# A Mamba mixer and gated MLP on one core: mixer input loaded by feature, x and B turned by DRAM blocks and VectorE

## The chip, the cores and the metric

The kernel runs on one core of one Trainium2 chip. The metric is device time in microseconds: the time of one execution as the device reports it, median of the runs. A profile of one execution (the hardware profiler's record) goes with it. TensorE is called PE, its weight load PEld, VectorE DVE, ScalarE ACT, GpSimd POOL and SyncE SP; SP issues nearly all DMAs.

## What is computed

`u` has 4 sequences of 1024 tokens with 256 features. Everything is float32.

```python
x = u
x = x + layernorm(mixer(layernorm(x)))
x = x + layernorm(mlp(layernorm(x)))

def mixer(u):                       # 8 heads of 64, state of 128
    z, xBC, dt = split(u @ in_proj) # 512 | 512 + 128 + 128 | 8
    x, B, C = split(silu(causal_conv4(xBC)))    # depthwise, over tokens
    dt = softplus(dt + dt_bias)
    dA = dt * -exp(A_log)
    # a linear recurrence over tokens, worked out in chunks:
    #   state = exp(dA) * state + dt * x B^T ;  y = C state + D * x
    y = y * silu(z)
    return rmsnorm(y) * norm_weight @ out_proj

def mlp(x):                         # 4-bit weights with scales per 32
    return (gelu(x @ Wg.T) * (x @ Wu.T)) @ Wd.T     # width 2048
```

The recurrence needs the transposed form of some operands. Projections and the convolution leave x, B and C by feature: features on partitions, tokens along the free axis. Two products of a chunk contract over tokens, so x (scaled by `dt`) and B are needed with tokens on partitions.

## The kernel before, in words

**Segments and chunks.** The 4096 tokens are cut into nine segments (line 26): two of 256 tokens, then seven of 512. A segment is cut into chunks of 128 tokens. For each segment `mixer(s)` (736) makes a list of steps and `ffn(s)` (1137) another.

**A planner sets the order.** No instruction is issued where the code stands. `Recorder.add` (181) notes each operation with what it reads and writes. `Recorder.issue` (288) then simulates the five engines, with a cost for each operation (`weigh`, 253), a rate and a fixed time for DMAs (344 to 349), a margin after each producer (`slack`, 142; 1.5 us after a DMA), and pools of buffers. At each step it takes, among the operations that can start soonest, the one of lowest rank (395), and so writes down a fixed order for each engine. That order is emitted at line 379, which is why every row of the profile says L379. On the chip each engine runs its list strictly in order and waits at each semaphore. Mixer steps of segment s + 2 rank ahead of the MLP of segment s, so that the two are interleaved.

**The mixer before the change.**
- `norm_in` (751): statistics of each token by DVE (`stats_of`, 594), the reciprocal deviation by POOL (`rstd_of`, 587), then for each chunk DVE writes `xn`, PE transposes its two halves into an `a` bank, and ACT copies the banks to `xnT`, which holds the normalized input by feature.
- `step_sizes` (767) and `decays` (818): dt, and the decay factors. The running sums by token go to DRAM (`rows`) and come back spread over partitions as `e` and `r`.
- `feature_pair` and `gate_pair` (1024, 1018), in segments from s = 4 on: input projections with seven products in place of eight (`pair`, 990), a Strassen scheme on 256x256 blocks. A pair occupies two of the four `f` banks of PSUM. The weights' sums come from DRAM (`win<-mstock`). Earlier segments use plain matmuls (`features`, 860).
- `convolve` (869): one ACT pass and three DVE passes from the bank into `xc`, then a tanh and a product that make silu.
- `inner(i)` (900), for each chunk: `e` and `r` are loaded, and exponentiated. PE transposes the four feature blocks of x into one bank (935 and 936), and DVE makes `xdt` and `xw` from it (939, 942). PE multiplies B by C, transposes B into the same bank (958), and ACT copies it to `bt` (960).
- `scan(i)` (1029): output from the state, update of the state from `bt` and `xw`, output within the chunk from `xdt` and `e`. Then `gated`, `way_out` and `turned` (1066 to 1111) end in `xfT`, the MLP's input by feature.

**The MLP.** `widen_pair` (1213) computes gate and up with the seven-product scheme (`seven`, 1189): PE writes into two `f` banks, ACT copies two halves on, DVE adds twice (`f<-f,sums`), PE goes on. This ring is the bulk of the work. Gelu and the product with up write the tile `big`; `narrow` (1221) multiplies by Wd into the `d` banks. Blocks of the weights' sums (1792 KB each) are fetched from DRAM by `fetch` (1171), `wide<-stock`, two buffers.

**Queues.** All loads and stores named here stand in SP's one list. SP waits at an issue until the buffer is free, and what is behind it in the list waits too.

Of the kernel before, what the change touches and what calls it, by code (L numbers as in the profile page):

```python
# [14 lines left out]
ALU = mybir.AluOpType  # L15
PSUM = bass.MemoryType.PSUM

P = 128
# [9 lines left out]
TMAX = 512  # L28
# [8 lines left out]
SIDE = 2  # L37
OUT = True
SEVEN = 4
MASKED = -2.0 ** 100  # L40

ATANH = (2.000000007877749, 0.6666631593507933, 0.400248537235466, 0.2796141883358907,
# [126 lines left out]
class Recorder:  # L169
# [118 lines left out]
    def issue(self, tc, rank, patience):  # L288


        steps = self.steps
        follows = [[] for _ in steps]
        for st in steps:
            st.missing = len(st.before)
            st.ready = st.floor
            st.rank = rank(st)
            for b in st.before:
                follows[b.at].append(st)
        open_ = {e: [] for e in self.ENGINES.values()}
        table = "exp"  # L300
        for st in steps:
            if not st.missing:
                open_[st.engine].append(st)
        free = {e: 0.0 for e in open_}
        wires = 0.0
        bundle = None
        order = []
        while len(order) < len(steps):
            best = None
            for e, sts in open_.items():  # L310
                when = {}
                for st in sts:
                    starts = [b.pool.may_start(b) for b in st.buffers]
                    if None not in starts:
                        when[st] = max(starts + [st.ready, free[e]])
                if e == "ACT" and when:


                    now = min(when.values())
                    other = [st for st in when if st.table not in (None, table)]  # L320
                    for st in other:
                        when[st] += SWITCH
                    if len(other) < len(when):
# [12 lines left out]
            t, st = best  # L336
            e = st.engine
            st.start = t
            if e == "ACT" and st.table:
                table = st.table  # L340
            turn = min(PORT, max(0.0, free["POOL"] - t)) if st.port and t < EARLY else 0.0
            free[e] = t + st.busy + turn
            st.end = free[e] + st.after
            if st.name == "dma_start":
                if st.bytes > 20000:
                    wires = max(free[e], wires) + st.bytes / (230.0 if st.repeats else 350.0)
                    st.end = wires + 1700.0
                else:
                    st.end = free[e] + 1900.0
            for b in st.buffers:  # L350
                if b.slot is None:
                    b.pool.take(b)
                b.left -= 1
                b.until = max(getattr(b, "until", 0.0), st.end)
                if not b.left:
                    b.pool.free.append((b.until, b.slot))
            if e == "PE":
                bundle = st.bundle
            open_[e].remove(st)
            order.append(st)  # L360
            for f in follows[st.at]:
                flows = f.before[st]
                if e == "PE" and f.engine == "PE":
                    r = st.start
                elif f.engine != e:
                    r = st.end + slack(e, f.engine)
                elif flows:
                    r = st.end
                else:
                    r = st.start  # L370
                f.ready = max(f.ready, r)
                f.missing -= 1
                if not f.missing:
                    open_[f.engine].append(f)
        self.order = order
        with tc.manual_schedule():
            for st in order:
                real = lambda a: a.on(a.buf.pool.slots[a.buf.slot]) if isinstance(a, View) else a
                getattr(getattr(self.nc, st.queue), st.name)(  # L379
                    *[real(a) for a in st.args], **{k: real(a) for k, a in st.kwargs.items()})  # L380
# [25 lines left out]
def mamba_ffn_kernel(  # L406
    ctx: ExitStack,
    tc: tile.TileContext,
    u: bass.AP,
    w_in: bass.AP,  # L410
    conv_w: bass.AP,
    conv_b: bass.AP,
# [18 lines left out]
    def pool(name, shape, k=1, ahead=2, of=None, dtype=F32):  # L431
        of = of or sb
        return Pool([of.tile(shape, dtype, name=f"{name}{j}") for j in range(k)], ahead)

    def fixed(name, shape, dtype=F32):
        return pool(name, shape, dtype=dtype).get()

    def given(ap):
        return Pool([ap]).get()

    u, w_in, conv_w, conv_b, dt_bias, a_log, d_skip, norm_w, w_out = map(
        given, (u, w_in, conv_w, conv_b, dt_bias, a_log, d_skip, norm_w, w_out))
    g_pack, g_scale, u_pack, u_scale, d_pack, d_scale, out = map(
        given, (g_pack, g_scale, u_pack, u_scale, d_pack, d_scale, out))

# [9 lines left out]
        "yo": pool("yo", [P, DI // P, P]), "xf": pool("xf", [P, 2, P], 2),  # L455
        "xfT": pool("xfT", [P, 2, TMAX], 2), "act": pool("act", [P, HALF], 3, 3),
        "fo": pool("fo", [P, DM], 2), "cst": pool("cst", [CMAX * NH, P], 2),
        "rows": pool("rows", [CMAX * NH, P], 2, of=hbm), "dec": pool("dec", [P, 3 * CMAX * NH], 2),
        "edge": pool("edge", [P, NF, 3], 2), "part": pool("part", [P, NF, 3], 2),
        **{k + who: pool(k + who, shape, 4, 4) for who in "mf"  # L460
           for k, shape in (("mv", [P, CMAX, 2]), ("st", [P, 6]), ("rs", [P, CMAX]))},
# [5 lines left out]
    def get(tag):  # L467
        return pools[tag].get()
# [107 lines left out]
    tails = [fixed(f"tail{b}", [P, NF, 3]) for b in range(NB)]  # L576

    big = [fixed(f"big{j}", [P, 2 * MLP]) for j in range(2)]

    def over_heads(v, n):  # L580

# [2 lines left out]
    def little(tag, n):  # L584
        return get(tag)[:, :n]

    def rstd_of(var, n, factor=1.0):

        v = get("rsm")[:, :n]
        r.gpsimd.tensor_scalar(v, var, factor, EPS * factor, ALU.mult, ALU.add)  # L590
        r.gpsimd.tensor_tensor(v, v, mhalf[:, :n], ALU.pow)
        return v

    def stats_of(rows, who="m"):

# [140 lines left out]
    def mixer(s):  # L736
# [7 lines left out]
        def ps_a():  # L744
# [3 lines left out]
                return (banks_a if v_.get("out") else banks_f).get()  # L748
            return (banks_d if s == 1 and v_["n"] % 2 else banks_a).get()

        def norm_in():
            x = v_["x"] = xs[s]
            mv = stats_of([x[:, i, :] for i in range(NC)])
            rs = rstd_of(mv[:, :, 1], NC)
            xnT = v_["xnT"] = by_segment(s, "xnT", lambda t, c: t[:, :, c])
            pT = [ps_a() for kk in range(2)]
            for i in range(NC):
                xn = get("xn")
                r.vector.tensor_scalar(xn, x[:, i, :], mv[:, i, 0:1], rs[:, i : i + 1],
                                        ALU.subtract, ALU.mult)  # L760
# [108 lines left out]
        def convolve(f, pp):  # L869
# [25 lines left out]
            th = get("th")[:, :T]  # L895
            r.scalar.activation(th, h, AF.Tanh)
            r.vector.scalar_tensor_tensor(h, th, 1.0, h, ALU.add, ALU.mult)


        def inner(i):  # L900
# [30 lines left out]
                j = i * NH + h  # L931
                r.scalar.activation(e_[:, h, :], raw[h], AF.Exp, bias=v_["ncs"][:, j : j + 1])

            px = ps_a()
            for f in range(4):
                r.tensor.transpose(px[:, f * P : (f + 1) * P], xc[:, f, tok], ident)
            px = px.rearrange("p (h c) -> p h c", c=HD)
            xdt = v_["xdt", i] = get("xdt")
            r.vector.tensor_tensor(xdt, px, over_heads(v_["dt"][:, hs], HD), ALU.mult)
# [8 lines left out]
            if t0 > 0 or i > 0:  # L948
                rr = v_["r", i] = get("r")
                by_pair = v_["rows"][hs, :].rearrange("(c two) t -> two c t", two=2)  # L950
                for k in range(2):
# [3 lines left out]
            pgb = ps_a()  # L955
            r.tensor.matmul(pgb[:, :P], lhsT=xc[:, 4, tok], rhs=xc[:, 5, tok],
                             start=True, stop=True)
            r.tensor.transpose(pgb[:, P : 2 * P], xc[:, 4, tok], ident)
            bt = v_["bt", i] = get("bt")
            r.scalar.copy(bt, pgb[:, P : 2 * P])  # L960
            r.vector.tensor_tensor(e_, e_, pgb[:, :P].unsqueeze(1).to_broadcast([P, NH, P]),
                                    ALU.mult)

# [173 lines left out]
    def ffn(s):  # L1137
# [73 lines left out]
            return one, two  # L1211

        def widen_pair(j):
            a = big[1][:, j % 4 * 2 * TMAX : (j % 4 + 1) * 2 * TMAX]
            for k, bank in enumerate(seven(0, j)):
                r.scalar.activation(a[:, k * TMAX : (k + 1) * TMAX], bank, AF.Gelu_apprx_tanh)
            for k, bank in enumerate(seven(1, j)):
                cols = slice(k * TMAX, (k + 1) * TMAX)
                r.vector.tensor_tensor(at[j % 4][:, cols], a[:, cols], bank, ALU.mult)
# [155 lines left out]
```

## Time and profile before

| | |
|---|---|
| median of 3 runs | 999.85 us (998.04 to 1000.05) |
| span of the profiled execution, first to last instruction | 995.4 us |
| the time around it, median less span | 4.45 us |
| PE, DVE, ACT, POOL busy | 983.0, 650.1, 517.0, 305.1 us |
| mean granted PE clock | 0.999 |
| DMA queue of SP | 110.78 MB, 33.8% of 16 DMA engines |
| PE transposes `a<-ident,xc` / `a<-ident,xn` | 148 / 58 |

A row of a profile's group reads: line, engine, operation, out<-in by the program's names, shapes, count, then busy time in all, the mean duration of one in ns, and the idle time of the engine before them with what ended it. In the names, `a`, `d` and `f` are PSUM banks; `wide` holds MLP weights or their sums; `big` the MLP's intermediate. Matmuls of float32 appear as two passes each, and their durations overlap.

### The profile page before, as it was taken

How to read it: one execution, taken by the hardware profiler on the slowest of the kernel's cores; microseconds unless marked ns; L12 is line 12 of the kernel's file. 1: busy time of each engine (PE TensorE's matmuls, PEld its weight loads, DVE VectorE, ACT ScalarE, POOL GpSimd, SP SyncE). 2: the span in 40 equal slices, each digit the busy share in tenths (PEclk: the TensorE clock that was granted, in tenths of full speed). 3: DMA queues.
4: the chain of work that ended last, by engine and by line, in shares of the span. 5: the costliest groups of instructions: out<-in, count | busy, mean ns of one | idle time of the engine just before them, and what ended most of it. 6: DMA issues, size and time to landing. Idle time of an engine off the chain costs nothing.

```text
span 995.4 us, 14948 instructions
## 1 busy us (share of the span) xinstructions
PE 983.0 (99%) x5275; PEld 813.7 (82%) x5275; DVE 650.1 (65%) x1412; ACT 517.0 (52%) x1289; POOL 305.1 (31%) x491
## 2 busy tenths in 40 slices
PE   8999999999999999999999999999999999999998
PEld 6788777877788878888888888888888888888886
DVE  4998576568666967787678754777467874432431
ACT  5645865447564764576457733576236762321321
POOL 2836654821250335024502431034310452001001
PEclk9999999999999999999999999999999999999999
DMA  6542153424423422354144423244233322422310
GB/s 203 110 112 91 78 167 117 170 64 139 163 76 98 131 81 92 127 159 156 43 145 142 157 75 106 91 136 153 76 116 132 98 102 96 148 74 95 107 43 21
DMA packets 48659, 111.76 MB, mean 112 GB/s; under 512 B 4664, under 2 KB 35768, under 8 KB 44472
## 3 DMA queue, kind: packets, MB, share of 16 engines
q1 hardware_dynamic: 48008, 110.78, 33.8%
q8 instruction: 41, 0.67, 0.3%
q14 instruction: 34, 0.28, 0.1%
q10 hardware_dynamic: 576, 0.02, 0.0%
HBM read 96.83 MB, written 13.96 MB: 111 GB/s over the span
## 4 chain that ended last, share of the span: by engine, by line
PE 94%; DVE 2%; POOL 1%; ACT 1%; issue 1%; POOLq 0%; DVEq 0%; ACTq 0%
PE f L379 48%; PE a L379 23%; PE d L379 23%; DVE xc L379 1%; DVE y L379 0%; DVE wide L379 0%; POOL sz L379 0%; ACT big L379 0%; DVE xn L379 0%; POOL y L379 0%; POOL rsf L379 0%; DVE yo L379 0%; POOL wd L379 0%; DVE e L379 0%; DVE big L379 0%
## 5 line engine op out<-in xcount | busy, mean ns | idle before, releaser
L379 PE MATMUL f<-wide 128*128 128x256 f32 x880 | 250.1, 382 | 0.1
L379 PE MATMUL f<-xfT,wide 128*128 128x256 f32 (+1 forms) x1024 | 248.4, 356 | 0.3 <-ACT big L379 0.2
L379 PE MATMUL d<-wd,big 128*128 128x256 f32 x992 | 248.0, 380 | 0.0
L379 PEld LDWEIGHTS d<-wd,big 128*128 128x128 f32 x992 | 183.6, 190 | 26.9 <-issue 4.1
L379 PEld LDWEIGHTS f<-xfT,wide 128*128 128x128 f32 x1024 | 171.2, 191 | 26.3 <-issue 5.9
L379 PEld LDWEIGHTS f<-wide 128*128 128x128 f32 x880 | 157.5, 190 | 32.2 <-issue 5.0
L379 DVE TENSOR_TENSOR f<-f,sums 128x256 f32<-128x256 f32 x216 | 92.4, 430 | 100.0 <-PE f L379 92.2
L379 POOL TENSOR_SCALAR_AFFINE_SELECT e<-e 128x1024 f32<-128x1024 f32 x31 | 35.3, 1137 | 201.5 <-DMA e<-rows 201.5
L379 ACT COPY f<-f 128x256 f32<-128x256 f32 x129 | 46.4, 362 | 93.0 <-PE f L379 70.4
L379 ACT ACTIVATE big<-f 128x512 f32<-128x512 f32 x108 | 63.1, 598 | 52.3 <-DVE f L379 40.8
L379 DVE TENSOR_TENSOR big<-big,f 128x512 f32<-128x512 f32 x108 | 73.2, 684 | 13.2 <-PE d L379 4.9
L379 ACT ACTIVATE e<-e,ncs 128x128 f32<-128x128 f32 x248 | 77.7, 392 | 5.2 <-POOL e L379 5.1
L379 DVE SCALAR_TENSOR_TENSOR xc<-f,cw,xc 128x511 f32<-128x511 f32 (+5 forms) x102 | 70.6, 713 | 1.8 <-ACT tail L379 0.4
L379 ACT ACT_TABLE_LOAD x52 | 66.7, 1283 | 4.3 <-issue 2.7
L379 PE MATMUL f<-xnT,win 128*128 128x256 f32 x240 | 66.1, 382 | 0.0
L379 POOL TENSOR_SCALAR rsf<-rsf 128x1 f32<-128x1 f32 x32 | 6.2, 193 | 187.1 <-ACT act L379 186.0
L379 PE MATMUL a<-wo,y 128*128 128x256 f32 x240 | 57.1, 381 | 0.0
L379 POOL TENSOR_TENSOR sz<-sz 128x256 f32<-128x256 f32 (+1 forms) x64 | 39.5, 619 | 35.5 <-ACT sz L379 34.2
L379 PEld LDWEIGHTS a<-wo,y 128*128 128x128 f32 x240 | 45.0, 190 | 6.3 <-DVE mvm L379 0.3
L379 PEld LDWEIGHTS f<-xnT,win 128*128 128x128 f32 x240 | 44.0, 190 | 7.2 <-ACT bt L379 0.8
L379 POOL TENSOR_TENSOR state<-state,dec 128x512 f32<-128x512 f32 x24 | 25.2, 1049 | 80.7 <-PE a L379 69.7
L379 DVE SCALAR_TENSOR_TENSOR fo<-d,rsf,x 128x256 f32<-128x256 f32 x30 | 14.3, 480 | 52.3 <-POOL rsf L379 52.2
(273 smaller groups left out, 1543.7 us busy)
## 6 DMA issues: line engine op xcount, KB each, us to landing
wide<-stock SPq DMA_DIRECT2D x28, 1792.0 KB, 7.3
e<-rows SPq DMA_DIRECT2D x31, 512.0 KB, 4.1
win<-mstock SPq DMA_DIRECT2D x25, 448.0 KB, 3.4
r<-rows SPq DMA_DIRECT2D x56, 128.0 KB, 4.6
stock<-sums SPq DMA_DIRECT2D x8, 512.0 KB, 2.6
out_dram<-fo SPq DMA_DIRECT2D x30, 128.0 KB, 1.7
x<-in_u_dram SPq DMA_DIRECT2D x7, 512.0 KB, 4.2
stock<-wide SPq DMA_DIRECT2D x6, 512.0 KB, 6.4
```

The source lines that it names most:

```text
L379: getattr(getattr(self.nc, st.queue), st.name)(*[real(a) for a in st.args], **{k: real(a) for k, a in st.kwargs.items()})
```

## The change

Three edits go together.

- `u` is passed a second time, transposed by the host into a tensor `u_t` of 256 rows by 4096 tokens. In the seven segments of 512 tokens, `norm_turned` loads the segment from it into `xnT`, by feature. Mean and reciprocal deviation, which exist by token on partitions, are stored to DRAM (`lines`, 4 bytes per piece), loaded back spread over all partitions into two `th` buffers, and subtracted by POOL and multiplied by DVE in place. The two smaller segments keep `norm_in`.
- In the last six segments (s from 3 on), `convolve` stores the five finished blocks of x and B to DRAM (`planes`, 640 rows of 512 tokens). For each chunk four DMAs fetch blocks of 32x32 into `blocked`, so that partition group c gets the tokens 32c to 32c + 31 of all 640 features, and one DVE transpose of 128x640 turns each block in its place. Its output `rows` is read in the place of the bank `px` and of `bt`. There is one `blocked` and two `rows`; they lie in the second half of `big[1]`.
- In return, the Gelu results of `widen_pair` have two rooms in `big[1]` where they had four.

The planner gets a rate of 130 bytes per ns for DMAs whose rows have at most 32 elements.

```diff
+TURNED = 3
+NX = 5 * P
...
                 if st.bytes > 20000:
-                    wires = max(free[e], wires) + st.bytes / (230.0 if st.repeats else 350.0)
+                    rate = 130.0 if st.shapes[0][-1] <= 32 else 230.0 if st.repeats else 350.0
+                    wires = max(free[e], wires) + st.bytes / rate
...
+        "planes": pool("planes", [5 * P, TMAX], 2, of=hbm),
+        "lines": pool("lines", [2, CMAX * P], 2, of=hbm), "dec": pool("dec", [P, 3 * CMAX * NH], 2),
...
     big = [fixed(f"big{j}", [P, 2 * MLP]) for j in range(2)]
+    blocked = big[1][:, MLP : MLP + NX]
+    by_rows = [big[1][:, MLP + (k + 1) * NX : MLP + (k + 2) * NX] for k in range(2)]
...
+        def norm_turned():
+
+
+            x = v_["x"] = xs[s]
+            r0, _ = rows_of(s)
+            mv = stats_of([x[:, i, :] for i in range(NC)])
+            rstd_of(mv[:, :, 1], NC, to=mv[:, :, 1])
+            xnT = v_["xnT"] = get("xnT")
+            r.sync.dma_start(out=xnT,
+                             in_=u_t[:, r0 : r0 + T].rearrange("(k p) t -> p k t", p=P))
+            lines = get("lines")
+            for k, op in enumerate((ALU.subtract, ALU.mult)):
+                r.sync.dma_start(out=lines[k].rearrange("(i p) -> p i", p=P), in_=mv[:, :, k])
+                by_token = get("th")
+                r.sync.dma_start(out=by_token, in_=lines[k].partition_broadcast(P))
+                (r.vector if k else r.gpsimd).tensor_tensor(
+                    xnT, xnT, by_token.unsqueeze(1).to_broadcast([P, 2, T]), op)
+
         def norm_in():
+            if s > 1:
+                return norm_turned()
...
             r.vector.scalar_tensor_tensor(h, th, 1.0, h, ALU.add, ALU.mult)
+            if s >= TURNED and f < 5:
+                if "planes" not in v_:
+                    v_["planes"] = get("planes")
+                r.sync.dma_start(out=v_["planes"][f * P : (f + 1) * P, :], in_=h)
...
-            px = ps_a()
-            for f in range(4):
-                r.tensor.transpose(px[:, f * P : (f + 1) * P], xc[:, f, tok], ident)
+            if s >= TURNED:
+                for c in range(4):
+                    at = i * P + 32 * c
+                    r.sync.dma_start(
+                        out=blocked[32 * c : 32 * c + 32, :].rearrange("p (g t) -> p g t", t=32),
+                        in_=v_["planes"][:, at : at + 32].rearrange("(g p) t -> p g t", p=32))
+                rows = by_rows[i % 2]
+                r.vector.transpose(rows, blocked)
+                px, bt = rows[:, : 4 * P], rows[:, 4 * P :]
+            else:
+                px = ps_a()
+                for f in range(4):
+                    r.tensor.transpose(px[:, f * P : (f + 1) * P], xc[:, f, tok], ident)
...
-            r.tensor.transpose(pgb[:, P : 2 * P], xc[:, 4, tok], ident)
-            bt = v_["bt", i] = get("bt")
-            r.scalar.copy(bt, pgb[:, P : 2 * P])
+            if s < TURNED:
+                r.tensor.transpose(pgb[:, P : 2 * P], xc[:, 4, tok], ident)
+                bt = get("bt")
+                r.scalar.copy(bt, pgb[:, P : 2 * P])
+            v_["bt", i] = bt
...
-            a = big[1][:, j % 4 * 2 * TMAX : (j % 4 + 1) * 2 * TMAX]
+            a = big[1][:, j % 2 * 2 * TMAX : (j % 2 + 1) * 2 * TMAX]
...
+        ("u_t", g["L0_attn_u"].reshape(NB * L, DM).T),
```

More of the change, by code (lines that the diff above doesn't have):

```diff
@@ L409, in mamba_ffn_kernel @@
     u: bass.AP,
+    u_t: bass.AP,
     w_in: bass.AP,
@@ L439, in given @@
         return Pool([ap]).get()
[L441 to L442 removed]
+    u, u_t, w_in, conv_w, conv_b, dt_bias, a_log, d_skip, norm_w, w_out = map(
+        given, (u, u_t, w_in, conv_w, conv_b, dt_bias, a_log, d_skip, norm_w, w_out))
     g_pack, g_scale, u_pack, u_scale, d_pack, d_scale, out = map(
@@ L457, in mamba_ffn_kernel @@
         "fo": pool("fo", [P, DM], 2), "cst": pool("cst", [CMAX * NH, P], 2),
-        "rows": pool("rows", [CMAX * NH, P], 2, of=hbm), "dec": pool("dec", [P, 3 * CMAX * NH], 2),
+        "rows": pool("rows", [CMAX * NH, P], 2, of=hbm),
+        "planes": pool("planes", [5 * P, TMAX], 2, of=hbm),
+        "lines": pool("lines", [2, CMAX * P], 2, of=hbm), "dec": pool("dec", [P, 3 * CMAX * NH], 2),
         "edge": pool("edge", [P, NF, 3], 2), "part": pool("part", [P, NF, 3], 2),
@@ L585, in little, with rstd_of @@
         return get(tag)[:, :n]
-    def rstd_of(var, n, factor=1.0):
+    def rstd_of(var, n, factor=1.0, to=None):
         v = get("rsm")[:, :n]
+        to = to or v
         r.gpsimd.tensor_scalar(v, var, factor, EPS * factor, ALU.mult, ALU.add)
-        r.gpsimd.tensor_tensor(v, v, mhalf[:, :n], ALU.pow)
-        return v
+        r.gpsimd.tensor_tensor(to, v, mhalf[:, :n], ALU.pow)
+        return to
     def stats_of(rows, who="m"):
```

## The prediction

> **What bounds the kernel now.** I read the page first (busy shares, then the chain that ended last), then the groups with their idle time, then a short timeline of TensorE, then the DMA rows.
>
> ```profile
> span 995.4 us, 14948 instructions
> ...
> PE 983.0 (99%) x5275; PEld 813.7 (82%) x5275; DVE 650.1 (65%) x1412; ACT 517.0 (52%) x1289; POOL 305.1 (31%) x491
> ...
> PE 94%; DVE 2%; POOL 1%; ACT 1%; issue 1%; POOLq 0%; DVEq 0%; ACTq 0%
> ...
> L379 DVE TENSOR_TENSOR f<-f,sums 128x256 f32<-128x256 f32 x216 | 92.4, 430 | 100.0 <-PE f L379 92.2
> ```
>
> TensorE is busy for all but 12.4 of 995.4 us and is 94% of the chain: the kernel ends when TensorE has run through its list. The DVE row tells who is late inside the seven-product ring: before its 216 adds DVE waits 92.2 us for PE, 0.43 us per add. So PE is the late one there, and DVE has 0.43 us in hand at each add. A saving on PE counts in full as long as nothing new spends that.
>
> A matmul's duration is its latency, not its price. The price is the distance from its start to the next start:
>
> ```profile
> 535.09 0.38 PE L379 MATMUL a<-ident,xc 128*128 128x128 f32 x2
> 535.31 0.60 PE L379 MATMUL d<-wd,big 128*128 128x256 f32 x2
> 535.74 0.38 PE L379 MATMUL a<-ident,xc 128*128 128x128 f32 x2
> 535.96 1.03 PE L379 MATMUL d<-wd,big 128*128 128x256 f32 x4
> ```
>
> Two transposes take 535.31 - 535.09 = 0.22 us, 0.11 each; two passes of a 128x256 matmul take 535.74 - 535.31 = 0.43, 0.216 each.
>
> **What goes.** `norm_turned` replaces `norm_in` in the seven segments of 512 tokens (s above 1): 8 transposes each, 56. From s = 3 on, 24 chunks lose four transposes of x and one of B, 120. Together 176 x 0.11 = **19.4 us of PE**. On ACT 14 `xnT` copies (0.590 each) and 24 `bt` copies (0.266), 14.7 us, and on DVE 28 `xn` (0.435), 12.2 us, go too. Both engines wait for PE, so I count nothing for them. Fewer products in the `a` banks are worth nothing either, PE never waits long for a bank.
>
> **What comes, on DVE.** 24 block transposes of 128x640. No row shows one. Bounds: 0.41 us (the 256-element `xf`) and 1.5 us (two passes at the rate of the next row); nearest is DVE `e<-e,a`, 1024 elements in 1.216 us, which gives 640 x 1.216 / 1024 = 0.76 us. The ring has 0.43 in hand, so each costs PE 0.76 - 0.43 = 0.33 us, 24 x 0.33 = **7.9 us**. At the lower bound it is 0, at the upper 24 x 1.07 = 26 us. `xdt` and `xw` then read SBUF in place of PSUM; `y<-y,sz`, from SBUF, takes 0.764 against 0.686 for `xdt`, 44 x 0.08 = 3.5 us of DVE, a few hundredths per add, counted at nothing. The seven multiplications of `xnT` (1024 elements, 1.2 us, 8.5 in all) stand where 12.2 us of `xn` stood: nothing. POOL gets seven subtractions, each twice `y<-xc,dsk` (1.039 us); it is 31% busy: nothing. The Gelu rooms fall from four to two; the multiplication that frees one stands on DVE before the next pair's adds, so no wait is added.
>
> [...]
>
> **What comes, on the queue.** Per segment from s = 3: five stores of planes (256 KB) and 16 block loads (80 KB, 640 pieces of 128 B). Per segment from s = 2: one load of 512 KB by feature, two stores of 512 pieces of 4 B, two broadcast loads of 256 KB. That is 161 more issues on SP, and 22.9 MB on 111.8, with the DMA engines at 33.8%. The volume hides. What matters is when the blocks land, since the transpose waits for them at the head of DVE's queue, with the ring's adds behind it, and PE waits for those.
>
> ```profile
> r<-rows SPq DMA_DIRECT2D x56, 128.0 KB, 4.6
> ...
> mstock<-win SPq DMA_DIRECT2D x3, 320.0 KB, 6.8
> ```
>
> ```profile
> q1 hardware_dynamic: 544, 0.26, 28.4%
> issues: line engine op xcount, KB each, median us to landing
> r<-rows SPq DMA_DIRECT2D x2, 128.0 KB, 2.9
> ```
>
> ```profile
> L379 SPq DMA_DIRECT2D mstock<-sums x5: 359/370/545, 180.7 to 205.4; - x5
> L379 SPq DMA_DIRECT2D mstock<-win x3: 1294/1671/1753, 72.8 to 75.8; - x3
> ```
>
> The first fence is the issue list, the second the window 553.2 to 557 us in which two `r` loads move alone, the third what an issue occupies SP (min/median/max ns). In the window 544 packets take 28.4% of 16 x 3.8 us: 32 ns each, for 512 B. In the first 5 us, ACT's queue moved 457 packets of under 100 B in 5.7% of 80 us: 10 ns each. A chunk's 2560 pieces are 160 per DMA engine, 1.6 to 5.1 us, beside the issuing. An issue takes 0.37 us with 512 pieces (`mstock<-sums`) and 1.67 with 640 (`mstock<-win`, behind 1.5 MB of other stores); `r` lands 2.9 us after an issue of 0.6, so 2.3 after its end. Four loads and the landing: 4 x 0.37 + 2.3 = **3.8 us**, at most 4 x 1.67 + 2.3 = **9.0 us**, at least 4 x 0.32 + 1.4 (the landing of `rows<-cst`) = 2.7.
>
> Against that stands the PE work which the planner's list, built from the changed code, puts between the fourth load and the transpose, at the slots above. In 12 of 24 chunks it is 5.6 to 6.5 us; in the other 12 it is 6.7 to 11.9, mostly with a weight load ahead in the queue (`wide<-stock` lands in 7.3 us). At 3.8 us nothing waits: **0**, the PE work of that window is the cover. At 9.0 the twelve short ones lack 2.9 us each, 35 us.
>
> Before the first block of a segment SP waits for its planes to land, with mixer weights queued behind. 2.2 to 3.7 us of PE work lie there, and `out_dram<-fo` (128 KB) lands in 1.7, `stock<-sums` (512 KB) in 2.6: about 2.1, covered. For the normalization, the window from the first store to the multiplication is 6 us and more, and the store (1.4 us as `rows<-cst`, 3.6 as `dsk`, which has 16 B pieces) and the broadcast (2.9 as `r`, 4.1 as `e`) take 4.3 to 7.7. I take 0.3 us for each of seven, **2 us**; from 0 to 7 x 1.7 = 12.
>
> [...]
>
> **Sum.** 995.4 - 19.4 + 7.9 + 2 = 985.9 us for the profiled execution. Its span is 995.4 and the median of the runs is 999.85, so 4.45 lies around it: **990.4 us**, forecast 990.
>
> **Rivals.** Less than 0.2% (2 us) can't be told from no change here.
>
> *All of it is gained.* The transpose is near 0.41 us and no load is late: 999.85 - 19.4 = 980. For it: the 92.2 us that DVE waits for PE. Against it: the wait for DMA at the head of DVE's queue is new. 0.20.
>
> *The slots come back as idle time.* The transposes wrote `a` banks and could run while the four `f` banks were held: a feature bank is held by one ACT pass (0.778) and three DVE passes (0.745 each), 3 us, times two. If such stretches are what limits, PE has lost a filler and not work: 999.85 within 4 us. For it: three feature pairs per segment each hold half of the `f` banks. Against it: PE is at 99 to 100% in each 100 us from 100 to 900. 0.15.
>
> *The block loads are late.* One mechanism, in the 12 chunks with short cover: DVE stands before its transpose, PE before DVE. At the upper price of 9.0 us, 999.85 - 19.4 + 35 = 1015. It makes the kernel slower than before as soon as four loads take longer than 6.1 + (19.4 - 7.9 - 2) / 12 = 6.9 us. For it: `mstock<-win`, the only row with 640 pieces, occupies SP for 1.67 us per issue. Against it: it stood behind other stores, and 512 pieces cost 0.37. 0.27.
>
> *The forecast* has the rest, 0.38. That the turn leaves TensorE is certain from the code: the 176 transposes are not in the new list.
>
> **Chances.** The second rival's 0.15 lies within 4 us of no change on either side, a third to each verdict. Faster: 0.38 + 0.20 + 0.05 = 0.63. Same: 0.05. Slower: 0.27 + 0.05 = 0.32. The range reaches from the full gain, 979, to just short of the worst late loads, 1014.
>
> **What would show it.** PE should show 176 fewer transposes and still be above 98% busy. The StreamTranspose rows on DVE should mean about 0.76 us, with little idle time before them put down to DMA; four block loads should take about 1.5 us of SP and land some 4 us after the first issue. I am wrong if DVE shows several us of idle time before each transpose released by the DMA of the planes (late loads), if it shows none and PE is idle while it waits for DVE or ACT in the `f` banks (a lost filler), or if the transpose itself takes 1.5 us.

## The result, and the profile after

The changed kernel takes 1095.62 us (median of four runs, 1093.52 to 1097.86); the kernel before takes 999.89 on the same chip (four runs, 998.04 to 1000.05). The ratio is 1.0961, with a 95% interval of 1.0941 to 1.0982: 96 us slower, where 990 was forecast with a range up to 1014.

From the page of the changed kernel, the lines that answer to those shown of before (span, busy time, chain by engine and by line, the adds of the seven-product ring, and the new multiplication of `xnT`):

```profile
span 1096.1 us, 14841 instructions
...
PE 993.9 (91%) x5099; PEld 813.2 (74%) x5099; DVE 674.8 (62%) x1415; ACT 509.0 (46%) x1255; POOL 325.8 (30%) x498
...
PE 74%; DMA 12%; DVE 7%; issue 3%; ACT 3%; POOL 2%; ACTq 0%; SPq 0%; POOLq 0%; DVEq 0%
PE f L382 39%; PE d L382 18%; PE a L382 17%; DMA lines<-mvm 8%; DMA th<-lines 3%; DVE xc L382 1%; DMA mstock<-sums 1%; ACT e L382 1%; DVE big L382 1%; DVE f L382 1%; DVE xw L382 1%; ACT L382 0%; DVE y L382 0%; DVE xdt L382 0%; POOL sums L382 0%
...
L382 DVE TENSOR_TENSOR f<-f,sums 128x256 f32<-128x256 f32 x216 | 91.8, 428 | 95.7 <-PE f L382 91.4
...
L382 DVE TENSOR_TENSOR xnT<-xnT,th 128x1024 f32<-128x1024 f32 x7 | 8.8, 1259 | 84.1 <-DMA th<-lines 84.1
```

The 176 transposes are gone (5275 to 5099 matmuls), and TensorE now stands idle for 1096.1 - 993.9 = 102.2 us where it stood 12.4. DMA makes 12% of the chain, where the chain of before shows none: 8% for the store `lines<-mvm` and 3% for the load `th<-lines`, the way of the statistics through DRAM, are most of it. VectorE waits 84.1 us ahead of seven multiplications that take 8.8.

The DMA rows of the same kernel (KB each, median us from issue to landing) name the one that is out of line. A store of 2 KB lands after 9.7 us; one of 16 KB lands after 1.5:

```profile
planes<-xc SPq DMA_DIRECT2D x30, 256.0 KB, 2.1
big<-planes SPq DMA_DIRECT2D x96, 80.0 KB, 4.3
th<-lines SPq DMA_DIRECT2D x14, 256.0 KB, 6.0
...
lines<-mvm SPq DMA_DIRECT2D x14, 2.0 KB, 9.7
rows<-cst SPq DMA_DIRECT2D x7, 16.0 KB, 1.5
```

The timeline of SyncE's queue around segment 3 shows how it adds up (start, us of issuing, transfer):

```profile
191.68 0.55 SPq L382 DMA_DIRECT2D lines<-mvm  x1
201.94 0.33 SPq L382 DMA_DIRECT2D th<-lines  x1
202.37 0.39 SPq L382 DMA_DIRECT2D lines<-mvm  x1
211.86 0.33 SPq L382 DMA_DIRECT2D th<-lines  x1
```

The queue stands before each load until the store has landed, and the second store is queued behind the first load. Store, load, store, load run in series: 216.92 - 191.68 = 25 us until the multiplication starts. VectorE and TensorE, in their timelines of the same stretch:

```profile
216.92 1.22 DVE L382 TENSOR_TENSOR xnT<-xnT,th 128x1024 f32<-128x1024 f32 x1 [17.60 <-DMA th<-lines]
```

```profile
218.29 1.08 PE L382 MATMUL a<-xnT,dtw 128*32 128x128 f32 x16 [13.66 <-DVE xnT L382]
```

The transfer itself is short. In the window 202.5 to 211.5 us, which holds one load and the second store, the DMA engines' busy tenths in 40 slices of 0.225 us are

```profile
DMA  0072589997550000000000000000000000000000
```

so the last packet moved some 2.7 us into the window, at 205.2 us, and the queue went on 6.7 us later, at 211.86. What happens in between the trace does not show.

The gap has a second price. In slices of 5 us (busy us of PE, PEld, DVE, ACT, POOL with counts, then granted clock, DMA share, GB/s):

```profile
200.00:205.00 5.00, 4.63 (x22) 3.74 (x20) 0.00 (x0) 0.29 (x1) 1.88 (x5) 1.00 0.30 53
205.00:210.00 5.00, 0.00 (x0) 0.00 (x0) 0.00 (x0) 0.00 (x0) 2.85 (x2) 0.80 0.02 0
210.00:215.00 5.00, 0.00 (x0) 0.00 (x0) 0.00 (x0) 0.00 (x0) 0.00 (x0) 0.50 0.42 8
215.00:220.00 5.00, 1.71 (x18) 1.26 (x19) 2.23 (x4) 0.27 (x1) 0.61 (x2) 0.50 0.37 97
220.00:225.00 5.00, 5.00 (x19) 3.23 (x18) 1.42 (x4) 1.10 (x3) 0.13 (x1) 0.83 0.00 0
```

The clock granted to TensorE falls to 0.50 while it is idle and is not yet whole in the slice after it resumes; over the span it is 0.951, against 0.999 before. So TensorE's busy time grew by 10.9 us although 19.4 us of slots had left it: a `d<-wd,big` product of two passes takes 1.22 us at 219.30, where the clock is 0.50, and 0.60 in the kernel before at 535.31, where it is 1.00. In slices of 0.5 us the clock is 1.00 up to 208.0, 0.54 in the slice from there and 0.50 until 221.5; it is 0.81 in the slice from 221.5 and 1.00 again from 222.0. So it fell some 3.4 us after TensorE stopped at 204.6, and came back some 3.4 us after it resumed at 218.3.

### The profile page after: what moved, and what is told of

Its sections match the earlier page's. It is cut to its first block, busy times and chain, and to the rows that moved or that the text cites. A ratio compares the mean times of both kernels' runs of the same rounds, so it can differ in the third digit from the quotient of the medians.

```text
span 1096.1 us, 14841 instructions
## 1 busy us (share of the span) xinstructions
PE 993.9 (91%) x5099; PEld 813.2 (74%) x5099; DVE 674.8 (62%) x1415; ACT 509.0 (46%) x1255; POOL 325.8 (30%) x498
## 3 DMA queue, kind: packets, MB, share of 16 engines
q1 hardware_dynamic: 126616, 133.89, 41.8%
## 4 chain that ended last, share of the span: by engine, by line
PE 74%; DMA 12%; DVE 7%; issue 3%; ACT 3%; POOL 2%; ACTq 0%; SPq 0%; POOLq 0%; DVEq 0%
PE f L382 39%; PE d L382 18%; PE a L382 17%; DMA lines<-mvm 8%; DMA th<-lines 3%; DVE xc L382 1%; DMA mstock<-sums 1%; ACT e L382 1%; DVE big L382 1%; DVE f L382 1%; DVE xw L382 1%; ACT L382 0%; DVE y L382 0%; DVE xdt L382 0%; POOL sums L382 0%
## 5 line engine op out<-in xcount | busy, mean ns | idle before, releaser
L382 PE MATMUL f<-wide 128*128 128x256 f32 x880 | 256.2, 391 | 5.6 <-ACT f L382 4.1
L382 PE MATMUL f<-xfT,wide 128*128 128x256 f32 (+1 forms) x1024 | 251.9, 359 | 4.2 <-DMA wide<-stock 3.8
L382 PEld LDWEIGHTS d<-wd,big 128*128 128x128 f32 x992 | 186.1, 191 | 29.0 <-issue 5.6
L382 PEld LDWEIGHTS f<-xfT,wide 128*128 128x128 f32 x1024 | 175.5, 193 | 33.0 <-issue 10.4
L382 PEld LDWEIGHTS f<-wide 128*128 128x128 f32 x880 | 160.8, 193 | 47.7 <-DVE f L382 8.7
L382 PE MATMUL f<-xnT,win 128*128 128x256 f32 x240 | 73.6, 416 | 29.7 <-DVE big L382 15.3
L382 PEld LDWEIGHTS f<-xnT,win 128*128 128x128 f32 x240 | 48.6, 210 | 39.7 <-DVE big L382 15.7
L382 DVE TENSOR_TENSOR xnT<-xnT,th 128x1024 f32<-128x1024 f32 x7 | 8.8, 1259 | 84.1 <-DMA th<-lines 84.1
L382 POOL TENSOR_TENSOR sz<-sz 128x256 f32<-128x256 f32 x64 | 39.7, 620 | 42.0 <-ACT sz L382 40.3
```

What stands on the lines that cost most here:

```text
L382: getattr(getattr(self.nc, st.queue), st.name)(*[real(a) for a in st.args], **{k: real(a) for k, a in st.kwargs.items()})
```

## Experiments

Each time is a median; each ratio is to the kernel before, run on the same chip beside it, with its 95% interval.

### Which part: blocks alone, norm alone

`e1_blocks` turns x and B by blocks and keeps the old norm in all segments:

```
         def norm_in():
-            if s > 1:
-                return norm_turned()
```

> All of the change but the normalization: norm_in stands again in every segment, the 24 block turns stay. Theory 1 (the slow part is the store of the statistics in pieces of 4 bytes, which lands 9.7 us after its issue in the changed kernel's profile, while DVE waits 84 us in all for what follows it): the loss is gone; 120 transposes of PE go, 13 us, and each DVE turn (0.84 us in the profile) costs at most 0.4 us over the slack, so 985 to 1000 us. Theory 2 (the block loads and turns are late or in the way): still 1040 us or more.

`e2_norm` has the new norm and no block turn:

```
-TURNED = 3
+TURNED = 99
```

> The normalization alone: u_t and the statistics by row as in the change, but x and B of every segment turned on TensorE as before. Theory 1: nearly all of the loss is here, 1080 to 1110 us, DVE again idle some 80 us before its multiplication of xnT. Theory 2: near the kernel before, 990 to 1000 us.

Measured: blocks alone 1003.7 (1.0041, 1.0026 to 1.0056), norm alone 1079.1 (1.0792, 1.0771 to 1.0813). The loss is mostly the norm's. By the ratios the two alone add up to 83 of the 96 us; the other 13 appear only when both stand together, and no run takes them apart. Blocks alone show a turn near the forecast 0.76 us, and no wait for the planes:

```profile
L382 DVE STREAM_TRANSPOSE big<-big 128x640 f32<-128x640 f32 x24 | 20.1, 836 | 0.0
```

But the gain that they should have brought, 13 us, is missing too. That question is taken up below.

### Why the norm: who waits, when, and for what

`e3_pool` puts both `xnT` operations on GpSimd, so that VectorE does not stand before one:

```
-                (r.vector if k else r.gpsimd).tensor_tensor(
+                r.gpsimd.tensor_tensor(
```

> The changed kernel with both operations on xnT on POOL: DVE no longer waits at the head of its list for the second broadcast load. If the wait costs because DVE stands (the ring's adds behind it), most of the loss goes: 1015 to 1040 us, and PE waits little. If it costs because the next segment's input comes late, or because SP stands between a store and its load, the time stays at 1080 us or more.

Measured: 1081.1 (1.0811, 1.0767 to 1.0854). Only 15 of 96 us go. TensorE still waits 32.4 us for `xnT`, now from GpSimd, so it matters little which engine stands at the head. The two other reasons of the expectation, an input that comes late and a queue that stands between store and load (102.5 us in all here, 99.6 in the changed kernel), this run does not tell apart.

`e4_told` leaves the data path and tells the planner, which wrote the order, that these stores end 9.7 us after their issue and not 1.9:

```
-                    st.end = free[e] + 1900.0
+                    small = st.space[0] != bass.MemoryType.DRAM and st.shapes[0][-1] == CMAX
+                    st.end = free[e] + (9700.0 if small else 1900.0)
```

> The changed kernel, its planner told that the store of the statistics ends 9.7 us after its issue in place of 1.9; nothing else. The data path is the same, only the order moves. Theory 1, price in the order: the planner puts other DVE and SP work into the wait, DVE's idle time before xnT falls from 84 us to below 25, 985 to 1015 us. If instead the longer chain itself is what counts (the next segment's input comes too late whatever the order), the time stays above 1040 us.

Measured: 1016.3 (1.016, 1.0139 to 1.0181). VectorE's wait ahead of the same seven multiplications:

```profile
L383 DVE TENSOR_TENSOR xnT<-xnT,th 128x1024 f32<-128x1024 f32 x7 | 8.8, 1254 | 11.9 <-DMA th<-lines 9.3 <-POOL xnT L383 2.7
```

84.1 us have become 11.9 with the same slow stores. Most of the loss is thus a late landing in an order that was written for an early one.

`e5_rows` turns the statistics with one TensorE transpose and stores eight rows of 512 B:

```
+            r.tensor.transpose(turned, mv.rearrange("p i k -> p (i k)"), ident)
...
+            r.scalar.copy(stat, turned)
+            r.sync.dma_start(out=lines, in_=stat)
...
-                r.sync.dma_start(out=lines[k].rearrange("(i p) -> p i", p=P), in_=mv[:, :, k])
```

> The whole change, but the statistics go to DRAM in 8 rows of 512 bytes: PE turns the 128x8 tile once per segment, ACT copies it, one store, then the two broadcast loads. Theory 1: the store lands in about 1.5 us as the store of the decay sums does, DVE's idle time before xnT falls below 20 us, 980 to 1000 us. Theory 2: 1050 us or more. A third theory (SP's wait between store and broadcast holds up the weight loads behind it, whatever DVE does) expects the same as theory 1, since that wait shrinks too.

Measured: 1017.5 (1.0185, 1.0158 to 1.0212). VectorE's wait ahead of the multiplication falls to 8.6 us, as theory 1 had it, but the time lies 17 us above that theory's range. What holds it up no run here shows; `e10_sixteen`, below, does without the extra transpose and is 12 us quicker.

`e6_probe` is blocks alone with 28 stores that nobody reads, of seven shapes:

```
...
+            if s > 1:
+                probe(i + s * NC, xdt[:, 0, :])
```

> The block turns alone (the earlier run at 1003.7 us), with 28 more stores to DRAM from data at hand that nobody reads or waits for, in seven shapes of four each: 256, 512 and 1024 pieces of 4 bytes side by side (b, a, g), 512 pieces of 4 bytes 64 and 512 bytes apart (c, d), 128 pieces of 16 and of 96 bytes (e, f). If the landing grows with the number of small pieces, g lands near 18 us, a near 9.7 and b near 5; if neighbours in one DRAM line wait for each other, d lands well below a; if any store of pieces that small is slow, e is as slow as a. The time tells whether such stores cost without a wait: no more than 2 us over 1003.7 if the wait alone is the price; 20 us or more if they hold up the queue.

The landings (KB each, median us), by shape: a is 512 neighbouring pieces of 4 B, b 256 of them, c 512 pieces of 4 B at 64 B from each other, d at 512 B, e 128 pieces of 16 B side by side, f 128 of 96 B (for g, 1024 neighbouring pieces, the trace gives no landing):

```profile
probeb<-xdt SPq DMA_DIRECT2D x4, 1.0 KB, 7.5
probec<-xdt SPq DMA_DIRECT2D x4, 2.0 KB, 2.5
probed<-xdt SPq DMA_DIRECT2D x4, 2.0 KB, 2.6
probee<-xdt SPq DMA_DIRECT2D x4, 2.0 KB, 2.6
probef<-xdt SPq DMA_DIRECT2D x4, 12.0 KB, 2.6
...
probea<-xdt SPq DMA_DIRECT2D x4, 2.0 KB, 9.2
```

Shape c has as many pieces, as small, as shape a. Neither number nor size of the pieces makes 9.2 us out of 2.5, but that several 4-byte pieces fall side by side.

The run took 1025.3 (1.0247, 1.0211 to 1.0282), 21.6 us over blocks alone. The queue shows why a store that nobody reads costs time. SyncE's queue at the third tile of segment 5, first in `e1_blocks`, then here:

```profile
482.93 0.34 SPq L382 DMA_DIRECT2D e<-rows  x1
485.10 1.95 SPq L382 DMA_DIRECT2D big<-planes  x4
```

```profile
484.57 0.45 SPq L382 DMA_DIRECT2D probeg<-xdt  x1
486.14 0.34 SPq L382 DMA_DIRECT2D e<-rows  x1
488.31 9.16 SPq L382 DMA_DIRECT2D big<-planes  x4
```

Behind the store, four block loads take 9.16 us to issue, where the same four take 1.95 without it. (Four loads right behind a `wide<-stock` of 1792 KB take longer in any case: 6.55 us at one place of `e1_blocks`, and 11.23 at the same place here, with a store g ahead.) VectorE waits 16.2 us in all for planes where it waited 0.0.

`e10_sixteen` is the whole change with pieces of 16 B: a token's place in DRAM is chosen so that the four values of a partition lie side by side, and the operand undoes it.

```
-            rstd_of(mv[:, :, 1], NC, to=mv[:, :, 1])
+            rs = rstd_of(mv[:, :, 1], NC)
+            mean = little("rsm", NC)
+            r.gpsimd.tensor_scalar(mean, mv[:, :, 0], 1.0, 0.0, ALU.mult, ALU.add)
...
-                r.sync.dma_start(out=lines[k].rearrange("(i p) -> p i", p=P), in_=mv[:, :, k])
+                r.sync.dma_start(out=lines[k].rearrange("(p i) -> p i", i=NC), in_=(mean, rs)[k])
...
+                by_tile = xnT.rearrange("q k (i p) -> q k i p", p=P)
...
+                    by_tile, by_tile, by_token.rearrange("q (p i) -> q i p", i=NC)
+                    .unsqueeze(1).to_broadcast([P, 2, NC, P]), op)
```

> The whole change, but mean and scale of each token are stored as 128 pieces of 16 bytes (a token tile's four values side by side) and read back through a rearranged operand; one small GpSimd copy more per segment. Theory 'landing of 4-byte neighbours': each store lands in about 2.6 us as the probe of that shape did, VectorE waits for th under 15 us in all where it waited 84, and the time is 1010 to 1025, like the version with one TensorE transpose of the statistics (1017.5). Rival 'two trips through DRAM, whatever their pieces': above 1045.

`e11_normonly` is the same without the block turn:

```
-TURNED = 3
+TURNED = 99
```

> The norm of the kernel just described alone, with x and B turned on TensorE throughout. Theory that the norm by feature, even with quick stores, makes the next segment's input late by its chain (statistics, store, load, GpSimd, VectorE): 1008 to 1020, while the first experiment (blocks alone) stands at 1003.7, so that the two parts nearly add up to the whole. Rival that the norm costs nothing once the stores are quick, and the two parts only get in each other's way in the queue: 995 to 1003.

Measured: the whole change 1005.2 (1.0066, 1.0044 to 1.0088), the norm alone 1001.6 (1.0017, 1.0001 to 1.0032). In the trace of the whole change the stores land in 1.8 us and the wait ahead of the multiplication is 6.9 us:

```profile
lines<-rsm SPq DMA_DIRECT2D x14, 2.0 KB, 1.8
```

```profile
L382 DVE TENSOR_TENSOR xnT<-xnT,th 128x1024 f32<-128x1024 f32 x7 | 14.2, 2035 | 6.9 <-POOL xnT L382 5.7 <-DMA th<-lines 1.2
```

The layout of 2 KB is worth 1.0961 - 1.0066 = 0.0895 of 1000 us, some 90 us of the 96, as long as the planner takes 1.9 us for the store in both. Against `e4_told`, whose order expects the late landing, the same layout is worth 9. That two trips through DRAM cost much in themselves falls. What is left, 7 us by the ratio (4 to 9 by the interval), is about the blocks' 4 us and the norm's 2.

### Where the gain of the removed transposes went

Four more versions, each written by the planner in the order that follows from its steps; of three of them, which also have the old norm, only the lines that matter are shown. `e7_noturn` is blocks alone without the VectorE turn (the loads write the turn's target, so x and B are not turned inside their blocks):

```
-                        out=blocked[32 * c : 32 * c + 32, :].rearrange("p (g t) -> p g t", t=32),
+                        out=rows[32 * c : 32 * c + 32, :].rearrange("p (g t) -> p g t", t=32),
...
-                r.vector.transpose(rows, blocked)
```

> The block turns alone, less the 24 turns on DVE: the block loads write the tile that xdt, xw and B are read from, so x and B are not turned within the blocks. If DVE's added work (0.84 us per turn, with 0.43 us in hand per add) eats the saving on PE, the time falls by some 10 us to 990 to 995. If the loads or the order are the cause, it stays within 3 us of 1003.7.

`e8_rooms` is the kernel before with the change's two Gelu rooms:

```
-            a = big[1][:, j % 4 * 2 * TMAX : (j % 4 + 1) * 2 * TMAX]
+            a = big[1][:, j % 2 * 2 * TMAX : (j % 2 + 1) * 2 * TMAX]
```

> The kernel before with two rooms for Gelu results in place of four, nothing else. If the lost rooms hold the ring up, 1005 us or more, which would explain why the block turns alone gain nothing; if not, within 2 us of before.

`e9_free` leaves out the turn of x and B from segment 3 on, in any form:

```
-                rows = by_rows[i % 2]
-                r.vector.transpose(rows, blocked)
-                px, bt = rows[:, : 4 * P], rows[:, 4 * P :]
+                px, bt = xc[:, i, :], xc[:, 4, tok]
```

> Leaves out, of the last six segments, the turn of x and B altogether: no TensorE transposes, no plane stores, no block loads, no VectorE turns; the products that follow take features as they lie, at the same sizes, so the values are not the reference's. The norm is the one of the kernel before. Theory 'traffic' (in the first experiment the stores and block loads cost what the transposes gave): 980 to 988, that is the kernel before less 13 to 19 us. Theory 'slots' (the transposes stood where TensorE would else have waited or run its next product later, so leaving them out gives nothing): 995 to 1002.

`e12_traffic` keeps the TensorE transposes beside the stores and block loads, which nobody reads:

```
-                rows = by_rows[i % 2]
-                r.vector.transpose(rows, blocked)
-                px, bt = rows[:, : 4 * P], rows[:, 4 * P :]
-            else:
-                px = ps_a()
-                for f in range(4):
-                    r.tensor.transpose(px[:, f * P : (f + 1) * P], xc[:, f, tok], ident)
+            px = ps_a()
+            for f in range(4):
+                r.tensor.transpose(px[:, f * P : (f + 1) * P], xc[:, f, tok], ident)
...
+            r.tensor.transpose(pgb[:, P : 2 * P], xc[:, 4, tok], ident)
```

> The kernel before with both Gelu rooms of the change, and in addition the change's plane stores (30) and block loads (96), whose data nobody reads; all TensorE transposes stay and VectorE turns nothing. Nothing of the output changes. Theory 'traffic': 1008 to 1016, since the traffic costs 10 to 15 us and nothing is given for it. Theory 'slots': 998 to 1003, the traffic itself costs under 3 us.

Measured: 1001.5 (1.0019, 1.0 to 1.0039), 999.5 (0.9989, 0.9974 to 1.0005), 1013.0 (1.014, 1.0121 to 1.016) and 1011.5 (1.0122, 1.0099 to 1.0145). The turn costs about 2 us, though the intervals with and without it overlap, and the rooms nothing. `e12_traffic` lies where theory 'traffic' had it. But leaving the work out altogether (`e9_free`) came out slower than doing it, which fits neither theory: each of these lists but that of `e8_rooms` stands in another order, and the order is part of the time. (`e8_rooms` has the order of before, instruction for instruction.)

So the next three runs keep the written order of before on every engine (and have the two Gelu rooms, which cost nothing). `e13_gap` leaves the 120 transposes of x and B out when the list is emitted, with nothing in their place:

```
+                step.left_out = s >= TURNED
...
+            step.left_out = s >= TURNED
```

> The kernel before in its own written order on every engine, with the 120 TensorE transposes of x and B of the last six segments left out and nothing in their place (the reads behind them take what lies in the bank, so the values are not the reference's). Theory 'order' (a removed transpose is worth its slot as long as the order around it stays): 984 to 989, 120 slots of 0.11 us less. Rival 'slots' (TensorE waits there, or runs its next product later): 996 to 1001.

`e14_dead` emits the change's stores and block loads into that order, behind and ahead of the steps that they belong to, and nobody reads them:

```
+            if s >= TURNED and f < 5:
+                step.behind.append(store_plane(s, f, h))
...
+            if s >= TURNED:
+                step.ahead.append(turn_tile((s - TURNED) * CMAX + i))
```

> The kernel before in its own written order, with the change's 30 plane stores and 96 block loads put into the queue and their data read by nobody; all transposes stay. Theory 'order': 998 to 1003, the traffic costs under 3 us. Rival 'traffic' (the 10 to 15 us of the version with dead traffic in an order of its own, 1011.5): 1008 to 1016.

`e15_kept` makes the whole block turn in that order. Other than its expectation says, the first tile of each of the six segments takes the B of the tile before it, since the copy of B stands ahead of the turn there. Beside the two diffs just shown:

```
+                nc.vector.transpose(real(by_rows), real(blocked[k % 2]))
...
+                step.instead[1] = rows
...
+                step.instead[1] = by_rows[:, 4 * P :]
```

> The turn by blocks alone, the norm as in the kernel before, written in the kernel before's order: stores after the feature, loads one token tile ahead, one VectorE turn of 128x640 ahead of the first product that reads it, transposes left out. It computes all that the reference asks. Theory 'order': 984 to 993, the transposes' 13 us less up to 6 for VectorE turns that come late for TensorE. Rivals 'slots' or 'traffic': 998 to 1012; the version in its own order took 1003.7.

`e16_patience` is the kernel before with one constant of the planner changed, same instructions in another order:

```
-PATIENCE = 30.0
+PATIENCE = 40.0
```

> The kernel before with the same instructions in another written order: the one constant by which the order lets a more urgent instruction start up to 30 ns later is 40 ns. Theory 'order' (the time depends on the written order by as much as was missed): 1003 to 1015. Rival (any order of these instructions is about as good): 998 to 1002.

Measured: `e13_gap` 993.9 (0.9953, 0.9941 to 0.9966), `e14_dead` 1011.4 (1.0125, 1.0109 to 1.014), `e15_kept` 1053.7 (1.0549, 1.0535 to 1.0563), `e16_patience` 1003.8 (1.0048, 1.0035 to 1.0061). In a fixed order the transposes are worth 4.8 us and not 13, between the two theories; another order of the same instructions costs 5; and dead traffic costs 12, which theory 'order' had at under 3. TensorE's waits in `e13_gap` have a row that those of `e8_rooms` have not (us in all, times, longest):

```profile
PE f L385 <- DVE f L385: 1.8, 6, 0.5
```

Where the largest piece of the 12 us comes from, some 7, the timelines show. In `e8_rooms` the three stores of the output have no loads ahead of them:

```profile
346.83 4.07 SPq L379 DMA_DIRECT2D out_dram<-fo  x3
```

In `e14_dead`, SyncE's queue, then VectorE, then TensorE:

```profile
345.08 6.38 SPq L601 DMA_DIRECT2D big<-planes  x12
351.56 3.28 SPq L385 DMA_DIRECT2D out_dram<-fo  x3
```

```profile
354.00 0.48 DVE L385 SCALAR_TENSOR_TENSOR fo<-d,rsf,x 128x256 f32<-128x256 f32 x1 [7.58 <-DMA out_dram<-fo]
```

```profile
354.88 1.22 PE L385 MATMUL f<-wide 128*128 128x256 f32 x2 [6.76 <-DVE f L385]
```

Twelve block loads stand ahead of three stores of the output and take 0.53 us each to issue. The `fo` buffer comes free only when its store has landed, VectorE stands for 7.58 us before it, and TensorE behind VectorE's ring for 6.76. The stores themselves landed 2.1 to 2.3 us after their issue, against 1.7 in the median, so nearly all of the wait is their place. The next pieces are smaller: TensorE waits 2.4 us once for ScalarE and 0.9 once for VectorE. In `e15_kept` the twelve loads take 7.00 us at the same place, VectorE waits for planes as well (36.3 us), and TensorE for VectorE (25.5 us): the order of before gives the blocks no time to land.

`e18_spread` is `e14_dead` with each block load put behind one transfer of the kernel's own:

```
+                if st.engine == "SP" and self.later:
+                    self.later.pop(0)()
```

> The kernel before in its own written order with the same 30 plane stores and 96 block loads, read by nobody, as the run with dead traffic that took 1011.4; but each block load is put behind one transfer of the kernel's own instead of up to twelve in a row. Theory 'place in the queue' (about 0.53 us of issue for each load, twelve of them ahead of a store that VectorE and TensorE wait behind): 999 to 1004. Rival 'traffic itself' (packets, DRAM, SBUF): 1008 to 1013.

`e17_act` is `e10_sixteen` with the block loads on ScalarE's queue:

```
-                    r.sync.dma_start(
+                    r.scalar.dma_start(
```

> The whole change with 16-byte pieces (1005.2), its 96 block loads issued from ScalarE's queue instead of SyncE's, in the order that follows from that. Theory 'place in the queue': 994 to 1002, as SyncE's queue is back to 30 plane stores and 28 transfers of the norm. Rival (ScalarE pays the issues, 2 us and more ahead of each tile's exponentials, or the order loses as much): 1003 to 1020.

Measured: `e18_spread` 1001.8 (1.0014, 1.0001 to 1.0027), `e17_act` 1019.9 (1.0201, 1.0176 to 1.0225). The same bytes cost 2 us when no store stands behind a row of loads, so the price is where the loads stand, not how many bytes they move. Spreading them also thins their packets in time, which this run does not tell apart from the place; and whether a kernel that reads the blocks could wait for loads so spread was not tried. Moving them to ScalarE is no remedy: that version is 14 us slower than `e10_sixteen` by the two ratios, TensorE waiting 11.1 us for VectorE in the `f` banks and 6.8 for ScalarE; how much of it is the order and how much the issues was not told apart. Of all versions only `e13_gap`, which leaves work out, is faster than before by more than its interval leaves open.

## Why the prediction was wrong, point by point

**The step that failed** is the landing of the statistics: "the store (1.4 us as `rows<-cst`, 3.6 as `dsk`, which has 16 B pieces) and the broadcast (2.9 as `r`, 4.1 as `e`) take 4.3 to 7.7. I take 0.3 us for each of seven, **2 us**; from 0 to 7 x 1.7 = 12." The store lands in 9.7 us, and neither row could show it: `rows<-cst` has pieces of 512 B, and `dsk` is a load. Besides, two pairs run in series and the step counted one: even with quick stores, 2 x (1.8 + 4.0) = 11.6 us lie between. That second slip alone costs little, as the norm alone with 16 B pieces stands 2 us over before. The term was 2 us and measured some 90. The list of what would show the forecast wrong did not name the sign that came, VectorE idle ahead of the multiplication of `xnT`; none of its three signs names that wait. That PE would stay above 98% busy failed too: 91%.

**What goes**: 176 slots of 0.11 us went, but "a saving on PE counts in full" does not hold. In the unchanged order 120 slots brought 4.8 us. Set side by side, product by product, `e13_gap` and `e8_rooms` have the same distance from most products to the next (216 ns in the median for those of 128x256). Sixty distances are longer in `e13_gap` by more than 50 ns, 9.8 us in all, and a few shorter, 2.8 us. Eleven of the sixty grew by 0.2 to 1.0 us, 5.1 us together, and there the trace shows TensorE waiting, nine times for VectorE and twice for ScalarE. The other 49 grew by some 0.1 us each where it shows no wait; what they are stays open. So part of the slots came back as short waits for the engines that read the banks, which is near the second rival's case.

**The VectorE turn**: 0.76 us was taken, 0.836 measured, with 1.5 us of idle time before all 24; the upper bound of 1.5 us was nearly twice too high. The charge of 7.9 us was too high as well: with and without the turn, blocks alone differ by 2 us.

**The block loads**: that nothing waits held for their data, but by less than it seemed. For the issuing of four, 4 x 0.37 = 1.5 us was taken; in the changed kernel it took 2.0 to 7.4 us, 3.5 in the median, and each load landed 4.3 us after its issue. The transpose began 5.9 to 12.6 us after the first of the four. What was missed is whom their issues hold up in SyncE's queue. The rival "the block loads are late" did not happen in the changed kernel.

**The planes' landing** (2.1 taken, 2.1 measured) and the Gelu rooms (nothing taken, nothing measured) were right.

**Not in the list at all**: the order is planned anew from the changed steps, and one constant of the planner alone moves the time by 5 us. A sum of steps can't see that, and a forecast of 10 us of gain stood on less than it seemed to. Two smaller figures were off without effect: the added traffic is 23.1 MB on SyncE's queue (110.78 to 133.89) and not 22.9, and the time around a span is 1.8 us in the changed kernel's profiled run (1097.86 against 1096.1) and not 4.45.

## What to carry to other kernels

When a small result goes through DRAM, look at how its pieces lie there: here 512 values of 4 B side by side landed 9.2 us after their issue, the same values at 64 B from each other after 2.5 and in pieces of 16 B after 2.6, and everything in a fixed order behind them stood. Where a planner writes that order, give it the measured landing: that alone took the loss from 96 us to 16. Price each new transfer twice, by who waits for its data and by who stands behind it in the queue. And where TensorE is 99% busy with a planned order, test a saved slot by leaving it out of the unchanged order before believing its price.

## What the runs showed of the hardware

- Stores of 512 neighbouring 4-byte pieces to DRAM landed 9.7 us (changed kernel, median of 14) and 9.2 us (`e6_probe`, median of four) after their issue, and stores of 256 such pieces 7.5 us (`e6_probe`), against 2.5 for 512 pieces at a pitch of 64 B; in the changed kernel's window from 202.5 us the last packet had moved 6.7 us before the queue went on. Four block loads behind a store of 1024 such pieces took 9.16 us to issue (`e6_probe`), and 1.95 at the same place without it (`e1_blocks`).
- Around six long gaps of the changed kernel (5.6 to 16.6 us), TensorE's granted clock fell to 0.50 some 3.0 to 5.0 us after it stopped and came back to 1.00 some 3.4 to 6.6 us after it last resumed.
- An operand read at a stride of 16 B made a 1024-element multiplication take 2.035 us on VectorE instead of 1.259 (`e10_sixteen`).
- VectorE turned 128x640 fp32 by 32x32 blocks in 0.836 us (`e1_blocks` and the changed kernel, mean of 24), 1.31 ns per element of a partition with all that is fixed.
